# A four-layer graph attention kernel: other all-node row blocks in layer 2, and the start of layer 3 tied behind layer 2's last row

## The chip, the cores and the metric

The kernel runs on one core of one Trainium2 chip. The metric is device time in microseconds (us) of one execution. Five engines work side by side, each in the order of its own instruction queue: PE (TensorE, matrix products), ACT (ScalarE, exponentials and copies), DVE (VectorE, elementwise work), POOL (GpSimd, which here issues gathers) and SP (SyncE, which issues plain DMAs). An instruction whose input is not there yet holds up everything behind it on the same engine.

## The reference

There are 4096 nodes with 256 features, an adjacency matrix with a density of about 1/256 plus the diagonal, and four graph attention layers. Each has a residual and a layer norm:

```
x = layernorm(x + layer_n(x, adj))          # n = 0, 1, 2, 3
layers 0, 1:  4 heads of 64;  layer 2: 2 heads of 128 (with biases)
   h = x W^T;  e[i,j] = leaky_relu(s1[i] + s2[j]) where adj[i,j], else excluded
   out[i] = softmax_j(e[i,:]) @ h
layer 3:  one score; softmax of e and softmax of -e (negated), both @ x,
   concatenated, @ fc_W, then elu
```

## The kernel before, in words

**Rows and tiles.** A tile of nodes is 128 rows, so there are NT = 32 row tiles, called row 0 to row 31 here. For each layer, a *projection* (class `Projection`, L526) turns a finished row into what the next layer needs of it: a value row for each node (`vals`) and its score terms (`edge`), both stored to DRAM. Its steps are a transpose on PE (`transpose`, L535), a copy of it on ACT (`copy`, xT, L543), the product on PE (L552), the scaling on ACT and DVE (`row`, L563, stored at L580), a transpose of the score terms (`edge`, L582) and their store (L588).

**Sparse rows.** Most row tiles are done sparsely (class `RowTile`). During layer 0 the kernel works out, for every row tile, a list of the neighbours that it has (`lists`), at most 13 x 128 of them, with packed masks (`maskC`). In every layer, a row tile then gathers 13 x 128 value rows with 13 indirect DMAs on POOL (L636), and its own 128 rows with a plain DMA on SP (L633). These 14 positions form two *halves* of seven (`half`, L640). Masked attention weights are made on ACT and DVE for each, and PE multiplies them with the gathered values (L711 in layers 0 and 1, L714 in layers 2 and 3). The lists are ordered so that the first six gathers touch only nodes of rows 0 to 16 (`MIX` = 17, `FRONT` = 6). The first half of a row tile of layer n+1 thus needs only the projections of rows 0 to 16; its second half needs those of all 32 rows. Gathered data goes to slots of two pools, `g0` (16 slots) and `g1` (14 slots). In layer 3 a position takes a whole slot, and in the other layers two positions share one. First halves use `g0`, and second halves `g1` (`place`, L609).

**All-node rows.** Some blocks of four row tiles are not done sparsely but against all 32 node tiles (`whole_rows`, L908). `WHOLE` (L98) gives the number of such blocks in each layer: three in layer 2 (rows 20 to 31) and one in layer 3 (rows 28 to 31). They are always the last blocks. One *unit* is the work of one block with one node tile: an exponential on ACT and a mask on DVE for 128 x 512 weights, and the matmuls (L953). Layer 2 has 96 units of two heads, layer 3 has 64 units of one sign each. Units need no gathers, only value rows and a mask read in order, so they are spread between the sparse halves. `whole` (L769) issues units in proportion to the half-steps done so far. The full masks of these blocks are saved in DRAM (`maskW`) by one store of 2.16 MB for each block (L392), while layer 0 runs.

**The order of the work.** The program is written out once in Python. The order in which it issues is the order of each engine's queue, except where the tile framework's scheduler moves instructions by their priority; `issue_after` makes it place instructions after a named one. In layers 2 and 3 a half-step (`half_with_whole`, L825) does the transpose of at most one finished row, a half of the current sparse tile, the rest of that projection, and its share of units. Finished rows wait in `ready`, in the order in which `norm` (L975) finishes them. `GROUPS` (L76) says how many consecutive rows share one layer-norm chain.

**The border of two layers.** `close` (L863) ends a layer. It projects those rows below 17 that are still in `ready`, asks for the gathers of the next layer's first tile, finishes the layer's last row, issues the first half of the next layer's tile 0, projects the remaining rows, and then handles the loads of tiles 1, 2 and 3 and the first half of tile 1. The next layer's first gather on POOL waits for the value stores of rows 0 to 16 and for free slots; the first gather of a second half waits for the stores of all rows.

**Banks.** PSUM is split into `ptwo` (two pairs), used for the sparse accumulators and for the projections of layers 1 and 3, and `pfour`/`pthree`, turns over the other banks, used for the units' accumulators and for the projections of layer 2.

Of the kernel before, what the change touches and what calls it, by code (L numbers as in the profile page):

```python
# [45 lines left out]
ALU = mybir.AluOpType  # L46
# [4 lines left out]
P = 128  # L51
N = 4096
F = 256
NT = N // P
KT = F // P
BT = 4
W = BT * P
NB = NT // BT
# [14 lines left out]
CAP = NG * P  # L73
HALF = NP // 2

GROUPS = (((24, 4),), ((28, 2),), ((16, 2), (20, 1), (31, 2)), ((28, 1), (31, 4)))  # L76
LEAD = 10
MIX = 17
FRONT = 6
# [15 lines left out]

WHOLE = (0, 0, 3, 1)  # L98

LEAST = 2.0611536224385579e-09  # L100

# [76 lines left out]
class Turns:  # L178


    def __init__(self, pools):
        self.pools = list(pools)
# [6 lines left out]
class Program:  # L189
# [98 lines left out]
    def lists(self, ctx):  # L288
# [75 lines left out]
        class Block:  # L364
# [23 lines left out]

            def places(self):
                blk = self.blk  # L390
                if blk >= NB - max(WHOLE):
                    nc.sync.dma_start(out=shared["maskW"][blk], in_=self.mk)  # L392
                hit = wk.tile([P, BT, NT], BF16, name="hit")
                nc.vector.tensor_scalar(hit, self.red, 0.0, None, op0=ALU.is_gt)
                flat = hit.rearrange("p t j -> p (t j)")
                nc.vector.memset(flat[:, blk * BT:blk * BT + (BT - 1) * (NT + 1) + 1:NT + 1], 0.0)
                pt = prog.bank(prog.pthree)
                nc.tensor.matmul(pt[:, :P], flat, ones, start=True, stop=True)
                totals = wk.tile([P, P], BF16, name="totals")
                nc.scalar.copy(totals, pt[:, :P])  # L400
                pq = prog.bank(prog.pthree)
                nc.tensor.matmul(pq[:, :P], tri, flat, start=True, stop=False, skip_group_check=True)
                nc.tensor.matmul(pq[:, :P], totals, bt.rearrange("p t j -> p (t j)"), start=False, stop=False,
                                 skip_group_check=True)
                nc.tensor.matmul(pq[:, P:P + BT], totals, tot, start=False, stop=True, skip_group_check=True)
                ms = slice(blk * BT, (blk + 1) * BT)
                self.place = wk.tile([P, BT, NT], F32, name="place")
                here = self.place
                nc.vector.tensor_tensor(here, pq[:, :P].rearrange("p (t j) -> p t j", t=BT), lo[:, ms, :],
                                        op=ALU.subtract)  # L410
                nc.vector.tensor_tensor(here, here, hit, op=ALU.mult)
                nc.vector.tensor_copy(total[:, ms], pq[:, P:P + BT])

                for col in (wid[:, ms, :], None):
                    off = wk.tile([P, BT, NT], F32, name="off")
                    if col is None:
                        nc.vector.tensor_scalar(off, here, 0.0, None, op0=ALU.is_lt)
                    else:
                        nc.vector.tensor_tensor(off, here, col, op=ALU.is_gt)
                    nc.vector.tensor_tensor(bad, bad, off, op=ALU.max)  # L420
# [105 lines left out]
class Projection:  # L526
# [54 lines left out]

    def edge(self):  # L582
        self.pe = self.prog.bank(self.banks[2])
        self.nc.tensor.transpose(self.pe[:TERMS[self.n], :P], self.terms[:, 0, :], self.shared["ident"])

    def store(self):
        n, nc, T = self.n, self.nc, TERMS[self.n]
# [12 lines left out]
class RowTile:  # L600

    def __init__(self, layer, m):
        self.layer, self.m = layer, m
        self.slots = {}
        self.accs = None

    def place(self, pos):  # L609


        L, n = self.layer, self.layer.n
        per = 1 if n == 3 else 2
        s = pos // per
        if s not in self.slots:
            pool = L.prog.g1 if n > 0 and s * per >= HALF else L.prog.g0
            self.slots[s] = pool.tile([P, 2 * ROW[0]], F32, name="G")
        c = (pos % per) * ROW[n]
        return self.slots[s][:, c:c + ROW[n]]
# [20 lines left out]
    def half(self, half):  # L640
# [1 line left out]
        prog, sh, S = L.prog, L.shared, self.S  # L642
        H, Wd, V, T, A = HEADS[n], WIDTH[n], VALS[n], TERMS[n], LOGS[n]
        if self.accs is None:
            pool = prog.ptwo[1 if n == 3 and self.m % 2 else 0]
            self.accs = [prog.bank(pool) for _ in range(2 if n == 3 else 1)]
        accs = self.accs
        G = [self.place(half * HALF + k) for k in range(HALF)]
# [88 lines left out]
class Layer:  # L737
# [2 lines left out]

    def __init__(self, prog, n):
        self.prog, self.n, self.nc, self.shared = prog, n, prog.nc, prog.shared
        self.count = NT - WHOLE[n] * BT
        self.tiles = {}
        self.loaded = set()
        self.units = self.whole_rows()
        self.total = WHOLE[n] * NT * (1 if n < 3 else 2)
        self.used = 0
        self.nxt = self.middle = self.stored = self.between = None
        self.group = []  # L750
        self.ready = []
        self.step = 0
        self.last = ()


    def tile(self, m):
        if m not in self.tiles:
            self.tiles[m] = RowTile(self, m)
        return self.tiles[m]

    def load(self, m, half):
# [4 lines left out]
    def set_banks(self):  # L766
        self.prog.banks = self.prog.ptwo[1] if self.n in (0, 2) else self.prog.pthree

    def whole(self, step):  # L769

        while self.between is None and self.used < self.total \
                and self.used < self.total * (step + 1) / (2 * self.count - 6):
            next(self.units)
            self.used += 1
        if self.used == self.total:
            next(self.units, None)

# [15 lines left out]
    def half_alone(self, m, part):  # L793


        self.step = 2 * m + part
        proj, middle = None, self.middle
        second = m > NT - (LEAD if self.n == 0 else 6) and len(self.ready) > 1
        if self.ready and self.ready[0][0] < self.step and (part == 0 or second):
            self.set_banks()  # L800
            if part == 1 and self.n == 0:
                self.prog.banks = self.prog.pthree
            proj = Projection(self.prog, self.n + 1, self.nxt, *self.ready.pop(0)[1:])
            proj.transpose()
        if part == 1 or self.tile(m).accs is None:
            self.tile(m).half(part)
        if self.stored is not None:
            self.stored.store()
        if proj is not None:
            proj.copy()  # L810
        if part == 0 and m >= 1:
            self.tile(m - 1).copy()
        if proj is not None:
            proj.multiply()
        if part == 0 and m >= 1:
            self.tile(m - 1).back()
        if middle is not None:
            middle.row()
        if part == 1 and m >= 1:
            self.tile(m - 1).finish()  # L820
        if middle is not None:
            middle.edge()
        self.stored, self.middle = middle, proj

    def half_with_whole(self, m, part):  # L825

        proj = None
        self.step = 2 * m + part
        if self.ready and self.ready[0][0] < self.step:
            _, y, row = self.ready.pop(0)  # L830
            self.set_banks()
            proj = Projection(self.prog, self.n + 1, self.nxt, y, row)
            proj.transpose()
        with ExitStack() as order:
            for ins in self.last:
                order.enter_context(self.prog.tc.issue_after(ins))
# [3 lines left out]
        if self.between is not None:  # L840

            self.last = self.between()
            self.between = None
        if self.stored is not None:
            self.stored.store()
            self.stored = None
        if proj is not None:
            proj.copy()
            proj.multiply()
        if part == (0 if self.n == 3 else 1) and m >= 1:  # L850
            self.tile(m - 1).finish()
        self.whole(2 * m + part)
        if proj is not None:
            proj.row()
            proj.edge()
            self.stored = proj

    def steps(self):
        for m in range(self.count):
            for part in range(2):  # L860
                self.part(m, part)

    def close(self, following):  # L863

        last = self.count - 1
        self.step += 2
        if self.stored is not None:
            self.stored.store()
        if self.middle is not None:
            self.middle.row()  # L870
            self.middle.edge()
# [3 lines left out]
            self.set_banks()  # L875
            Projection(self.prog, self.n + 1, self.nxt, *entry[1:]).all()
        if following is not None:
            following.load(0, 0)
        if WHOLE[self.n]:
            for _ in self.units:  # L880
                pass
            self.tile(last).finish()
            if following is not None:
                following.tile(0).half(0)
        else:
            self.set_banks()
            first = Projection(self.prog, self.n + 1, self.nxt, *self.ready.pop(0)[1:])
# [7 lines left out]
            self.tile(last).finish()  # L895
            first.edge()
            first.store()
        for _, y, m in self.ready:
            self.set_banks()
            Projection(self.prog, self.n + 1, self.nxt, y, m).all()  # L900
        if following is not None:
            for m in (1, 2):
                following.load(m, 0)
# [4 lines left out]
    def whole_rows(self):  # L908
        n, nc, prog, sh = self.n, self.nc, self.prog, self.shared
        H, Wd, T = HEADS[n], WIDTH[n], TERMS[n]  # L910
        groups = [range(H)] if n < 3 else [(0,), (1,)]
        for blk in range(NB - WHOLE[n], NB):
            tiles = range(blk * BT, (blk + 1) * BT)
            S = prog.bk.tile([P, T, BT, P], F32, name="Sw")
            for it, m in enumerate(tiles):
# [59 lines left out]
    def norm(self, y, m):  # L975
# [24 lines left out]
            nc.vector.tensor_scalar(u, u, -0.5, 1.5, op0=ALU.mult, op1=ALU.add)  # L1000
            nc.vector.tensor_tensor(r, r, u, op=ALU.mult)
        for i, (y, m) in enumerate(self.group):
            nc.vector.tensor_scalar(y, y, mv[:, i, 0:1], r[:, i:i + 1], op0=ALU.subtract, op1=ALU.mult)
            dst = self.prog.out if self.n == 3 else self.shared["x"][self.n + 1]
            nc.sync.dma_start(out=dst[m * P:(m + 1) * P, :], in_=y)
            if self.n < 3:
# [498 lines left out]
```

## Time and profile before

| what | value |
|---|---|
| median of 3 runs | 2269.56 us (2267.93 to 2270.27) |
| the profiled execution's own time | 2264.38 us |
| its span in the profile | 2262.6 us |
| mean granted TensorE clock | 0.963 |
| PE busy | 2017.9 us (89%) |
| DVE busy | 1786.5 us (79%) |
| ACT busy | 1733.8 us (77%) |
| POOL busy | 1501.8 us (66%), of it 1488.8 in 1456 gathers |
| DMA moved | 493.01 MB, 218 GB/s on average |

The span is that of one execution, from its first instruction to its last, and all times inside the profile count from its start. "Busy" is the sum of instruction times on one engine. Projection and lists of layer 0 fill the first part. The last gathers of layer 2 are issued at 1681.56 us, the first of layer 3 at 1739.22 us. In the view of waits, a line reads: engine, tile and line that waited, what released it, total us, how often, and the longest.

### The profile page before, as it was taken

What the parts mean: (1) busy time and instruction counts of PE and PEld (TensorE: products, weight loads), DVE (VectorE), ACT (ScalarE), POOL (GpSimd) and SP (SyncE); (2) the same over time, 40 slices, a digit from 0 to 9 for tenths busy, and PEclk for the clock granted to TensorE, in tenths of its full rate; (3) what the DMA queues carried; (4) which work ended last, traced back from release to release, by engine and by line L of the source; (5) the groups of instructions that cost most, each with busy time, mean ns of one, the idle gap of its engine ahead of it and who ended that gap; (6) DMA issues with size and microseconds to landing.
All of it is one profiled execution on the core that took longest, in us unless ns stands there. A gap on an engine that the chain in (4) does not pass through costs nothing.

```text
span 2262.6 us, 49121 instructions
## 1 busy us (share of the span) xinstructions
PE 2017.9 (89%) x15689; PEld 1834.8 (81%) x15689; DVE 1786.5 (79%) x5061; ACT 1733.8 (77%) x4977; POOL 1501.8 (66%) x1596
## 2 busy tenths in 40 slices
PE   4878888989999969998898898999998899999996
PEld 2658777878999859988888898989996688778885
DVE  2988899999999859988888886886975455575566
ACT  4778988988789849978888877987873666686664
POOL 2117556656777777777777777777751677777773
PEclk7999999999999979999999999999999999999998
DMA  8889778776466665665656656777764788888884
GB/s 281 260 262 330 243 221 297 246 240 226 143 172 190 180 192 173 182 180 166 180 168 170 179 169 184 215 221 228 219 200 147 244 262 281 267 269 272 268 248 139
DMA packets 250321, 493.01 MB, mean 218 GB/s; under 512 B 44385, under 2 KB 156610, under 8 KB 249666
## 3 DMA queue, kind: packets, MB, share of 16 engines
q0 software_dynamic: 81536, 245.30, 37.3%
q1 hardware_dynamic: 168514, 244.46, 33.6%
q8 instruction: 126, 2.06, 0.4%
q14 instruction: 145, 1.19, 0.2%
HBM read 437.05 MB, written 52.54 MB: 216 GB/s over the span
## 4 chain that ended last, share of the span: by engine, by line
PE 48%; DVE 18%; DMA 15%; ACT 8%; issue 7%; POOL 3%; SPq 1%; DVEq 0%; ACTq 0%; POOLq 0%
PE bank L714 15%; PE bank L711 15%; DMA G<-vals,idx 8%; PE bank L953 8%; DVE w L670 6%; PE bank L552 4%; PE bank L441 4%; ACT w L699 3%; POOL G L636 3%; DMA raw<-in_adjB_dram 3%; DVE w L691 2%; DVE oh L435 2%; DMA G<-vals 2%; ACT pw L942 1%; ACT mk L380 1%
## 5 line engine op out<-in xcount | busy, mean ns | idle before, releaser
L636 POOL DMA_INDIRECT G<-vals,idx x1456 | 1488.8, 1023 | 722.6 <-issue 236.1
L699 ACT ACTIVATE w<-S,G 128x128 f32<-128x128 f32 x3248 | 1001.8, 390 | 144.9 <-DMA G<-vals,idx 105.5
L711 PE MATMUL bank<-w,G 128*65 128x128 f32 x7168 | 838.9, 277 | 61.1 <-DVE w L670 60.9
L711 PEld LDWEIGHTS bank<-w,G 128*65 128x65 f32 x7168 | 799.7, 140 | 71.0 <-DVE w L670 69.9
L670 DVE SCALAR_TENSOR_TENSOR w<-w,bank 128x1792 f32<-128x1792 f32 x256 | 514.4, 2012 | 15.0 <-ACT w L699 12.6
L714 PE MATMUL bank<-G,w 128*128 128x257 f32 (+1 forms) x2688 | 495.4, 342 | 30.4 <-DVE w L679 14.2
L714 PEld LDWEIGHTS bank<-G,w 128*128 128x128 f32 x2688 | 435.4, 194 | 80.9 <-DVE w L679 16.9
L953 PE MATMUL bank<-vw,pw 128*128 128x129 f32 (+1 forms) x2048 | 299.3, 302 | 5.3 <-ACT zw L1017 2.7
L953 PEld LDWEIGHTS bank<-vw,pw 128*128 128x128 f32 x2048 | 275.0, 192 | 21.9 <-ACT zw L1017 3.1
L677 ACT ACTIVATE w<-S,G 128x128 f32<-128x128 f32 x392 | 138.1, 393 | 138.3 <-DMA G<-vals 74.3
L435 DVE TENSOR_SCALAR oh<-iota,place 128x256 bf16<-128x256 f16 (+2 forms) x992 | 222.5, 300 | 10.1 <-PE bank L441 9.9
L691 DVE TENSOR_TENSOR w<-S,G 128x256 f32<-128x256 f32 x384 | 151.6, 416 | 70.5 <-DMA G<-vals,idx 67.4
L441 PE MATMUL bank<-mk,oh 128*128 128x132 fp8e4 x2336 | 189.9, 225 | 15.9 <-ACT cm L448 7.8
L552 PE MATMUL bank<-wext,xT 128*128 128x268 f32 (+3 forms) x640 | 180.6, 415 | 21.5 <-ACT xT L543 18.7
L441 PEld LDWEIGHTS <-oh 128*128 128x128 bf16 x2336 | 145.5, 98 | 52.0 <-DVE oh L435 15.6
L380 ACT ACTIVATE mk<-raw 128x1024 uint8<-128x1024 int32 x128 | 130.5, 1051 | 30.3 <-DMA raw<-in_adjB_dram 28.5
L552 PEld LDWEIGHTS bank<-wext,xT 128*128 128x128 f32 x640 | 118.5, 202 | 42.7 <-ACT xT L543 22.8
L943 DVE SCALAR_TENSOR_TENSOR pw<-pw,mw 128x512 f32<-128x512 f32 x192 | 127.4, 689 | 15.2 <-ACT pw L942 14.3
L942 ACT ACTIVATE pw<-Sw,d 128x512 f32<-128x512 f32 x192 | 133.1, 710 | 7.5 <-DMA Sw<-edge 5.3
L950 DVE TENSOR_TENSOR pw<-pw,mw 128x512 f32<-128x512 f32 x64 | 43.9, 689 | 112.4 <-ACT pw L949 57.9
L701 DVE SCALAR_TENSOR_TENSOR w<-w,mk 128x896 f32<-128x896 f32 x80 | 86.7, 1087 | 48.8 <-ACT w L699 48.6
L448 ACT ACTIVATE cm<-bank 128x396 uint8<-128x396 f32 (+1 forms) x160 | 68.8, 452 | 45.7 <-PE bank L441 44.4
(130 smaller groups left out, 1534.5 us busy)
## 6 DMA issues: line engine op xcount, KB each, us to landing
raw<-in_adjB_dram SPq DMA_DIRECT2D x128, 512.0 KB
mk<-maskC SPq DMA_DIRECT2D x112, 231.0 KB
G<-vals,idx POOLq DMA_INDIRECT x1456
S<-edge SPq DMA_DIRECT2D x64, 256.0 KB
vw<-vals SPq DMA_DIRECT2D x96, 129.0 KB
xp<-y SPq DMA_DIRECT2D x96, 128.0 KB
y<-xp SPq DMA_DIRECT2D x96, 128.0 KB
mw<-maskW SPq DMA_DIRECT2D x20, 528.0 KB
```

The costliest lines, as they stand in the source:

```text
L380: nc.scalar.activation(mk[:, q:q + 2, :, :P], src, AF.Copy, scale=EDGE)
L435: nc.vector.tensor_scalar(oh[:, :n * P], iota[:, :n * P], self.place[:, it, j:j + 1], None, op0=ALU.is_equal)
L441: nc.tensor.matmul(accs[b][:, s * MC:(s + 1) * MC], oh[:, (k - a) * P:(k - a + 1) * P], mk[:, j, it, :].bitcast(FP8), start=touches[b][0] ...
L552: nc.tensor.matmul(pp[:, :c1 - c0], self.xT[:, k, :], wext[:, k, c0:c1], start=(k == 0), stop=(k == KT - 1 and brow is None))
L636: nc.gpsimd.indirect_dma_start(out=self.place(pos), out_offset=None, in_=sh["v"][n][:NODES[t], :], in_offset=bass.IndirectOffsetOnAxis(ap= ...
L670: nc.vector.scalar_tensor_tensor(pair, pair, LEAST, mh2, op0=ALU.max, op1=ALU.mult)
L691: nc.vector.tensor_tensor(w[h][:, k:k + 2, :], S[:, h:h + 1, :].to_broadcast([P, 2, P]), dd[:, :, V + T + h:V + T + h + 1].to_broadcast([P ...
L699: nc.scalar.activation(w[h][:, k, :], S[:, h, :], AF.Exp, bias=d(k, h))
L711: nc.tensor.matmul(accs[0][:Wd, h * P:(h + 1) * P], v, w[h][:, k, :], **how)
L714: nc.tensor.matmul(a, w[h][:, k, :], v, **how)
L942: nc.scalar.activation(p, S[:, h], AF.Exp, bias=d)
L953: nc.tensor.matmul(accs[it][:, c:c + Wd], p[:, it, :], v[:, c:c + Wd], start=(j == 0 and h == heads[0]), stop=(j == NT - 1), skip_group_ch ...
```

## The change

`WHOLE` becomes a list of blocks for each layer. Layer 2's all-node blocks are 3, 7 and 6 in this order (rows 12 to 15, 28 to 31, 24 to 27) in place of 5, 6 and 7; its sparse rows are now 0 to 11 and 16 to 23. `GROUPS` follows that order, and `maskW` is saved for blocks 3, 6 and 7. Layer 3's all-node block stays block 7. In `half_with_whole`, rows below 17 are projected before others, and once the layer's units are used up two rows may be projected in one half-step, in its last three tiles. In layer 3, slots now alternate between the two pools by tile, with the second and third pairs arranged so that four first halves can be loaded at once. `close` loads four first halves of layer 3, projects what is ready, issues five of layer 3's units ahead of the last row's finish, and ties tile 0's first half and five more units behind the last row's scaled result and its projection's last transpose. The other 54 units of layer 3 are spread as before.

```diff
-GROUPS = (((24, 4),), ((28, 2),), ((16, 2), (20, 1), (31, 2)), ((28, 1), (31, 4)))
+GROUPS = (((24, 4),), ((28, 2),), ((16, 2), (17, 1), (20, 2), (24, 1), (31, 2)), ((28, 1), (31, 4)))
-WHOLE = (0, 0, 3, 1)
+WHOLE = ((), (), (3, 7, 6), (7,))
+AHEAD = 10
+ORDER = tuple([m for m in range(NT) if m // BT not in w] for w in WHOLE)
...
-                if blk >= NB - max(WHOLE):
+                if any(blk in w for w in WHOLE):
                     nc.sync.dma_start(out=shared["maskW"][blk], in_=self.mk)
...
     def place(self, pos):
...
-            pool = L.prog.g1 if n > 0 and s * per >= HALF else L.prog.g0
+            if n == 3:
+                other = self.step % 2 == 0 if self.step > 3 else self.step > 1 and s < HALF
+            else:
+                other = n > 0 and s * per >= HALF
+            pool = L.prog.g1 if other else L.prog.g0
...
     def whole(self, step):
         while self.between is None and self.used < self.total \
-                and self.used < self.total * (step + 1) / (2 * self.count - 6):
-            next(self.units)
-            self.used += 1
+                and self.used < self.ahead + (self.total - self.ahead) * (step + 1) / (2 * self.count - 6):
+            self.unit()
...
     def half_with_whole(self, m, part):
-        proj = None
+        projs = []
         self.step = 2 * m + part
-        if self.ready and self.ready[0][0] < self.step:
-            _, y, row = self.ready.pop(0)
-            self.set_banks()
-            proj = Projection(self.prog, self.n + 1, self.nxt, y, row)
-            proj.transpose()
+        able = sorted((e for e in self.ready if e[0] < self.step), key=lambda e: e[2] >= MIX)
+        self.set_banks()
+        over = self.used == self.total and m > self.count - 4
+        for entry, banks in zip(able, (self.prog.banks, self.prog.pthree)[:1 + over]):
+            self.ready.remove(entry)
+            projs.append(Projection(self.prog, self.n + 1, self.nxt, *entry[1:], banks=(banks,) * 3))
+            projs[-1].transpose()
...
     def close(self, following):
...
         if following is not None:
-            following.load(0, 0)
+            for m in range(4 if following.n == 3 else 1):
+                following.load(m, 0)
         if WHOLE[self.n]:
             for _ in self.units:
                 pass
+            if following is None:
+                self.tile(last).finish()
+                return
+            following.ahead = AHEAD
+            self.project_ready()
+            for _ in range(AHEAD // 2):
+                following.unit()
             self.tile(last).finish()
-            if following is not None:
+            scaled = self.scaled
+            proj = self.project_ready()
+            with ExitStack() as order:
+                for ins in (scaled, proj.last):
+                    order.enter_context(self.prog.tc.issue_after(ins.ins))
                 following.tile(0).half(0)
+                for _ in range(AHEAD - AHEAD // 2):
+                    following.unit()
...
-        for blk in range(NB - WHOLE[n], NB):
+        for blk in WHOLE[n]:
```

`project_ready` projects all rows in `ready` one after the other and gives back the last projection; its `last` is the transpose of the score terms in `edge`, and `self.scaled` is the last instruction of `norm` that scales a row.

## The prediction

> **What bounds the kernel now.** I read the page first, then the windows around the border between layers 2 and 3, where the diff acts, then the chain of waits there, then POOL's timeline. The page's busy totals and two rows of its slices:
>
> ```profile
> PE 2017.9 (89%) x15689; PEld 1834.8 (81%) x15689; DVE 1786.5 (79%) x5061; ACT 1733.8 (77%) x4977; POOL 1501.8 (66%) x1596
> ...
> PE   4878888989999969998898898999998899999996
> ...
> POOL 2117556656777777777777777777751677777773
> ```
>
> No engine is full over the whole span; the slices tell more. PE is near full from the middle on, but POOL, which does little but issue gathers, falls to 5 and 1 in slices 30 and 31 (56.6 us each, 1640 to 1753), the end of layer 2. The windows there (columns: length, busy and count of PE, PEld, DVE, ACT, POOL, granted clock, DMA share, GB/s):
>
> ```profile
> 1700.00:1720.00 20.00, 20.00 (x155) 19.01 (x154) 19.93 (x114) 7.20 (x25) 0.00 (x0) 1.00 0.34 102
> 1720.00:1740.00 20.00, 16.56 (x91) 12.98 (x90) 10.05 (x50) 3.55 (x12) 0.78 (x1) 0.92 0.36 110
> 1740.00:1760.00 20.00, 12.96 (x49) 9.62 (x50) 6.11 (x16) 11.40 (x29) 14.21 (x16) 0.82 0.82 268
> ...
> 1780.00:1800.00 20.00, 11.15 (x40) 8.73 (x39) 5.21 (x8) 11.94 (x26) 15.18 (x16) 0.83 0.78 243
> ...
> 2040.00:2200.00 160.00, 160.00 (x741) 140.24 (x740) 95.95 (x285) 104.03 (x220) 123.84 (x119) 1.00 0.85 265
> ```
>
> PE is full to 1720 and has holes to 1800; the DMA engines are a third used while POOL is still, four fifths once it gathers. Two waits of 1690 to 1830 and POOL's timeline:
>
> ```profile
> POOL G L636 <- DMA y<-xp: 56.7, 1, 56.7
> ACT w L677 <- DMA G<-vals,idx: 27.9, 23, 6.0
> ```
>
> ```profile
> 1681.56 0.95 POOL L636 DMA_INDIRECT G<-vals,idx  x1 [0.30 <-issue]
> 1739.22 0.94 POOL L636 DMA_INDIRECT G<-vals,idx  x1 [56.72 <-DMA y<-xp]
> 1740.47 0.95 POOL L636 DMA_INDIRECT G<-vals,idx  x1 [0.30 <-issue]
> ```
>
> POOL stands 56.7 us. The releaser named, a load of y, was long done; what comes just before 1739.22 is the value store of node row 16, issued at 1735.38 (L580). Layer 3 has 28 sparse tiles of 13, 364 gathers, from 1739.22 to 2234.4: 1.36 us each, where 0.95 busy and 0.30 issue give 1.25. In 2040 to 2200 it is 160/119 = 1.345 with PE full too, so gathers and PE run in step and neither makes up a late start. After the last gather 28.2 us remain. Layer 3 ends a fixed stretch after its gathers get under way.
>
> PE's holes at the border, off its timeline: between 1728.14 and 1754.22, while projections run singly, 1.07, 0.52, 0.95, 0.52, 0.95, 0.52, 2.23, 2.97 and 0.41; then 0.89, 7.65 and 1.72 to 1800.52: 20.4 in all. The lower clock adds some 5.6: a projection's multiply (L552) took 3.46 and 3.81 us for 2.01, a half's matmuls (L714) 8.58 for 6.23.
>
> **What the Trainium skill says.** "TensorE: Matmul & The Clock Gate", What's actually happening: throttled is the default, and activity releases the clock. The trace agrees: 0.82 and 0.83 in the windows with holes, 1.00 in full ones. "Perfetto Trace Analysis", DMA Instruction — SWDGE (GPSIMD): a gather's profiled end is that of descriptor writing, not of the data. The trace agrees: bars of 0.95 us, landings 3.2 to 5.8 us after issue. "DMA: Bandwidth & Descriptors", Issuing engines are not separate DMA queues: SP's and POOL's transfers share 16 engines. That bears on the moved mask store below; the trace's share of 0.99 there fits.
>
> **The change part by part.** Sums are on the profiled execution, 2264.4 us (span 2262.6); the median of 2269.56 is 5.2 above it.
>
> *Early rows first.* A layer-3 tile's first six gathers touch node rows 0 to 16 only. Rows 12 to 15 now belong to layer 2's first unit block, and projections of rows under 17 go ahead of others, so row 16's store comes before the last sparse tiles instead of after them. 24 gathers (first halves of four tiles, two in each slot pool) now stand ahead of the first full-range one: 24 x 1.25 = 30 us into POOL's hole of 56.7. What hides them is that hole and the DMA share of 0.34; without it they'd cost what they cost now. They wait for slots that layer 2 frees tile by tile, the last three for its last half.
>
> *Two projections a step.* After the last layer-2 unit (1700.1) both orders have six sparse halves (3.13 us of PE each) and ten projections (2.07 each). Before, four lie between the halves, and the last half ends 28.0 us on. Now seven lie between: about 28.0 + 3 x 2.07 = 34.3, so 1734.3, or 1736.9 with a few short xT waits of 0.5 to 1 us. Then three projections (6.2) and five layer-3 units (1.735 each, 8.7), which fill the last row's finish (5.1 to 5.4 us on DVE, PE idle before). The last row's edge transpose, call it t, comes at about 1750 if nothing stalls.
>
> *What queues behind the tie.* ACT has tile 0's and 1's relus (L677), which wait for gathers as late as the 22nd and for own rows over SP, ahead of the last xT copies; DVE has a mask of tile 1 ahead of the last row's reciprocal and eight unit multiplies (0.69 each) ahead of its value product; PE has five units ahead of its transposes. Behind all three waits row 23's projection, its store and the 25th gather, the first that may touch any row. A relu waited up to 6.0 us here, and a copy held so left PE idle 2.97. Bounds 0 and 8.5 us (6.0 and a multiply or two queue): t is 1750 to 1758.5. I take 1757.5; a hold is likely.
>
> *From t on.* The store and issue took 3.8 us (1735.38 to 1739.22), so the 25th gather is at about t + 3.5, against 1775.99. Gathers 27 to 54 then wait for the halves of tiles 0 and 1 to free slots: half 6.1, five units 8.7, half 6.1 give t + 21; gathers of tile 1's second half to t + 27, landing 4 to 5, masks 2.3 and half 6 give about t + 40; seven more gathers at 1.25 put the 55th at t + 46 to 49, I take 46.4, against 1816.4. Gain: 1816.4 - 1750 - 46.4 = 20.0, or 11.5 with t = 1758.5, 12.5 with 1757.5. The 310 gathers left at 1.353 (460 us / 340 in 1776 to 2236) are 419, with the tail 28: t + 494. PE has 56 x 6.07 + 59 x 1.735 = 442 left after t, and with the 15 us tail ends by t + 457 plus its idle (32 of 493 us before): no later.
>
> *Steady layer 3.* Slots alternate by tile, not by half, with a look-ahead of two tiles as before. 54 units over 50 steps for 64: ten units, 17 us of PE, leave the stretch. If PE paces it, up to -5; if smaller units interrupt more, +3. I take 0.
>
> *The mask store* (L392, 2.16 MB) of block 5 at 372 us becomes one of block 3 at about 200:
>
> ```profile
> 200.00:220.00 20.00, 18.10 (x172) 17.04 (x170) 19.42 (x66) 15.76 (x43) 15.43 (x16) 0.91 0.99 326
> 220.00:240.00 20.00, 13.80 (x145) 13.36 (x143) 12.92 (x39) 16.24 (x41) 9.69 (x11) 0.83 0.99 353
> ```
>
> The engines are full there and DVE loses 7 us in the second window, waiting for raw loads and what follows. 2.16 MB at 340 GB/s is 6.4 us; queued ahead of a raw load on SP, it delays all of it or, hidden, none. At 372 DVE idled 2.7 us, regained. Net -2.7 to +6.4; I take +2.5.
>
> *Other order.* Unit weights of layer 2 now start from rows 12 to 15, so eight exponentials (0.71 on ACT) and multiplies (0.69 on DVE) move some tiles earlier at layer 1's end, where both engines have them to do anyway: 0, within 2 either way. The other norm groups have the same rows: 0.
>
> Sum: -12.5 + 2.5 + 0 = -10, so 2254.4 profiled and 2259.5 median.
>
> **Rivals.** *The hole closes wholly:* nothing holds t (1750), the mask store is hidden and the clock stays up: -20 to -25, about 2247. For it: DMA share 0.34 and PE full to 1720; against it: relus and copies in one queue.
>
> *The gain is eaten:* t near 1765, or t as taken and the mask store at its full price with 3 to 5 us lost in the paced halves: within 0.2% (4.5 us, about what this kernel's measurement can tell from no change), 2268. For it: the seven gathers of each half must land before its relus, twice in a row.
>
> *Slower:* the tie itself. If each of the three holds behind one another (own row over SP, 22nd gather, units' multiplies) costs the 8.1 us that DVE waited for ACT's pw here at the longest, t is 1750 + 24.3 = 1774. From t = 1770 the 55th gather is no earlier than before; 4 us beyond, with the store's 2.5, gives +6.5: 2276. For it: three engines wait in order; against it: 24 gathers need only 30 us of the hole.
>
> *It doesn't happen:* front gathers stay behind the last tile's slots, POOL's hole stays 50 us or more. Gathers 1 and 2 have free slots, so only partly; it ends as the second rival.
>
> **How the numbers follow.** My case 0.50 (-4.5 to -18), hole closed 0.20, eaten 0.14, slower 0.16. The range runs from just past the closed hole, 2244, into the slower case, 2273; my case alone is 2252 to 2265. Faster 0.70, same 0.14, slower 0.16.
>
> **What would show it.** Right: POOL busy over 10 us in the 20 us windows of 1700 to 1740; the 25th gather at 1753 to 1762; the 55th at 1796 to 1805; PE holes between 1728 and 1800 under 10 us; steady gathers still 1.35 apart; the last gather 28 us before the end. Wrong: ACT's relu waits ahead of an xT copy over 6 us; raw waits over 6 us longer at 200 to 240; or a stretch before 1680 that shifts by more than 4 us.

## The result

The changed kernel takes 2261.25 us (median of 7 runs, 2253.32 to 2264.68). The kernel before took 2267.40 us in the runs beside it (median of 7, 2263.02 to 2270.27). The ratio is 0.9973, with a 95% interval of 0.9959 to 0.9987: faster by 0.27%, or 6 us, where 10 were forecast. The two profiled executions differ by 3.1 us (spans of 2262.6 and 2259.5). Single executions of one kernel lie up to 9 us from their median here, so one pair of traces shows where time went, and the medians show how much.

The page of the changed kernel, with the rows that were shown of the kernel before:

```profile
PE 2020.2 (89%) x15689; PEld 1842.9 (82%) x15689; DVE 1786.0 (79%) x5061; ACT 1730.1 (77%) x4977; POOL 1493.1 (66%) x1596
...
POOL 2107656656667777777777777777773477777773
```

The work is the same, but POOL's hole has moved its weight: 7, 3 and 4 in slices 30 to 32 for 5, 1 and 6. The windows at the border, with the columns as in the prediction:

```profile
1700.00:1720.00 20.00, 18.05 (x129) 16.56 (x128) 19.55 (x98) 18.98 (x51) 6.78 (x8) 1.00 0.76 221
1720.00:1740.00 20.00, 15.39 (x96) 13.50 (x95) 11.03 (x56) 4.41 (x15) 5.62 (x6) 0.91 0.70 199
1740.00:1760.00 20.00, 17.19 (x87) 14.68 (x86) 12.88 (x39) 9.44 (x18) 1.93 (x3) 0.91 0.51 146
1780.00:1800.00 20.00, 19.66 (x91) 16.96 (x90) 9.99 (x13) 17.29 (x37) 13.52 (x13) 1.00 0.77 238
2040.00:2200.00 160.00, 149.59 (x675) 128.63 (x674) 93.43 (x284) 98.95 (x214) 124.04 (x119) 0.99 0.83 253
```

From 1740 on PE is fuller than before (17.19 for 12.96, 19.66 for 11.15). Between 1700 and 1740 it is emptier (33.4 us busy for 36.6), although it has more to do there. In 2040 to 2200 it is no longer full, yet the same 119 gathers are issued: 1.345 us each, as before. The waits of 1690 to 1830, and POOL's timeline around the first gather that may touch any row:

```profile
POOL G L645 <- PE bank L723: 30.4, 23, 9.6
ACT w L686 <- DMA G<-vals,idx: 30.0, 16, 6.6
...
POOL G L645 <- DMA vals<-row: 22.9, 1, 22.9
```

```profile
1743.91 0.95 POOL L645 DMA_INDIRECT G<-vals,idx  x1 [0.30 <-issue]
1767.78 0.94 POOL L645 DMA_INDIRECT G<-vals,idx  x1 [22.93 <-DMA vals<-row]
```

The single wait of 56.7 us has become some twenty for slots (released by matmuls of layer 2), and one of 22.9 us for the last row's value store. *Front gathers* are here the 24 of the first halves of tiles 0 to 3, which touch rows 0 to 16 only; a *full-range* gather may touch any row. All 24 front gathers are out at 1743.91; the 25th gather, the first full-range one, waits for the store alone.

In the kernel before, POOL's timeline has the first full-range gather in 21st place, with four front gathers behind it that are issued before the 25th:

```profile
1770.85 1.08 POOL L636 DMA_INDIRECT G<-vals,idx  x1 [4.24 <-issue]
1775.99 0.95 POOL L636 DMA_INDIRECT G<-vals,idx  x1 [0.30 <-issue]
```

No releaser is named, but POOL's queue stood there in a wait of 8.8 us that ended at 1770.14, 4.1 us after the last row's value store was issued. The last edge transposes of the two kernels, on PE, first before and then changed:

```profile
1765.83 0.27 PE L584 MATMUL bank<-ident,row 128*1 128x128 f32 x1
1764.09 0.27 PE L587 MATMUL bank<-ident,row 128*1 128x128 f32 x1 [0.95 <-DVE row L581]
```

The last row's projection itself thus came only 1.7 us earlier.

The gather stream allows a simple account, which I use for every run below. It counts layer 3's gathers 1 to 364 in the order of POOL's queue and calls the last gather of layer 2 gather 0. *Border* is the time from the start of gather 0 to the start of the 25th, *stream* from there to the start of the last gather, *tail* from there to the end of the span. All three come from POOL's timelines of single executions.

| kernel | border | stream | tail | sum |
|---|---|---|---|---|
| before | 94.4 | 457.5 | 29.2 | 581.0 |
| changed | 86.8 | 457.6 | 34.1 | 578.5 |

The border gave 7.6 us. The stream did not move at all: in both kernels POOL waits only 3.5 and 6.2 us in it beyond the 0.30 between two gathers, so the issue of gathers itself sets its length. The tail took 4.9 us back. Kernels with the same order of work differ by 2 to 3 us in their border (experiments 2 and 8), so these are sizes to within about that. The two sums differ by 2.5 us of the 3.1; the rest lies ahead of gather 0. The eight kernels of the first chips that have the changed order of layer 2 issue gather 0 at 1674.6 to 1682.6, on average 2.7 us before the 1681.56 of the one trace of the kernel before; whether a part of the gain in the medians lies there, no run separates.

### The profile page after: what moved, and what is told of

Its sections match the earlier page's. It is cut to its first block, busy times and chain, and to the rows that moved or that the text cites. A ratio compares the mean times of both kernels' runs of the same rounds, so it can differ in the third digit from the quotient of the medians.

```text
span 2259.5 us, 49108 instructions
## 1 busy us (share of the span) xinstructions
PE 2020.2 (89%) x15689; PEld 1842.9 (82%) x15689; DVE 1786.0 (79%) x5061; ACT 1730.1 (77%) x4977; POOL 1493.1 (66%) x1596
## 5 line engine op out<-in xcount | busy, mean ns | idle before, releaser
L686 ACT ACTIVATE w<-S,G 128x128 f32<-128x128 f32 x392 | 137.2, 391 | 148.6 <-DMA G<-vals 94.6
L688 DVE TENSOR_TENSOR w<-w,mk 128x896 f32<-128x896 f32 x56 | 61.0, 1090 | 96.3 <-ACT w L687 87.6
```

The lines of the kernel that those rows point to most:

```text
L686: nc.scalar.activation(w[0][:, k, :], S[:, 0, :], AF.Relu, bias=d(k, 0))
```

## The experiments

All kernels were timed beside the kernel before on the same chip, so two kernels are compared by their ratios to it. The first eight ran on chips where that took 2267.05 and 2267.08 us. The last four ran on one where it took 2768.77; they are told apart below. "No difference" means that the intervals, 2 to 5 us either way, overlap.

**1. Tile 1's relus behind the last projection.** ACT's timeline of the changed kernel shows what the last projections met (L686 are relus of layer 3, L573 the exponential of a projection's row, L546 a projection's copy):

```profile
1723.29 0.40 ACT L686 ACTIVATE w<-S,G 128x128 f32<-128x128 f32 x1 [4.28 <-DMA G<-vals,idx]
...
1734.16 0.40 ACT L686 ACTIVATE w<-S,G 128x128 f32<-128x128 f32 x1 [5.05 <-DMA G<-vals,idx]
1734.47 0.45 ACT L573 ACTIVATE row<-bank 128x2 f32<-128x2 f32 x2
```

A relu of tile 1 stands for 4.28 and again for 5.05 us until its gather has landed, and the rows of two projections go right after it, at 1734.47. The gather it waits for is itself late, since its slot comes free with layer 2's halves. The tie of the change holds tile 0's half on DVE and PE only: an instruction is placed behind a named one on that one's engine, and the two named are on DVE and PE. Tile 0's relus and their two followers indeed stand on ACT from 1710.58 on, ahead of all these projections. Tile 1 isn't tied at all. The edit, all else as changed:

```diff
-        nc.scalar.activation(vals[:, :, D:], sc[:, 2 * T:2 * T + H].rearrange("p (h o) -> p h o", o=1), AF.Exp)
+        self.exp = nc.scalar.activation(vals[:, :, D:], sc[:, 2 * T:2 * T + H].rearrange("p (h o) -> p h o", o=1), AF.Exp)
...
+        tied = ()
...
+                tied = (scaled, proj.last, proj.exp)
...
-            following.tile(1).half(0)
+            with ExitStack() as order:
+                for ins in tied:
+                    order.enter_context(self.prog.tc.issue_after(ins.ins))
+                following.tile(1).half(0)
```

> The changed kernel with layer 3's tile 1 tied behind the last row's projection on ACT, DVE and PE (nothing is left out). Theory (in-order holds): tile 1's relus, which wait for late gathers, stood in ACT's queue ahead of the last four projections and made layer 2's last halves and the last edge transpose some 10 to 14 us late (1764.1 instead of about 1750). Without them PE's holes of 3.5 and 2.8 us before 1750 go, the last edge transpose comes at 1752 to 1757, the first full-range gather at 1756 to 1761 instead of 1767.8, and the end is 5 to 10 us earlier than the changed kernel (some 2252 to 2256). Rival (gathers or the SP queue pace layer 3 whatever the border does): the border moves but the end stays within 2 us of the changed kernel. Second rival: the relus' 5 us of ACT work are then exposed after the last row, and the first gather gains under 4 us.

Measured: 2249.02 us, ratio 0.9922 (0.9905 to 0.9939), against the changed kernel's 0.9973. In its account the border is 79.6, the stream 456.7 and the tail 34.2. POOL's timeline:

```profile
1735.15 0.94 POOL L645 DMA_INDIRECT G<-vals,idx  x1 [0.30 <-issue]
1754.56 0.94 POOL L645 DMA_INDIRECT G<-vals,idx  x1 [18.47 <-DMA vals<-row]
```

Counted from gather 0 (1674.91 here, 1681.02 in the changed kernel), the last edge transpose comes at 76.1 us instead of 83.1, and the 25th gather moves by the same 7.1. The stream passes it on to the end in full. The holes of 3.48 and 2.81 us that PE had in the changed kernel before 1750 are gone too. So the hold is shown, and its price is 7 us of the border; the medians differ by some 12, of which the trace accounts for 7.9. Both rivals fall.

**2. Output stores behind the own-row loads.** The tail of the changed kernel, on PE, on SP and in ACT's waits of 2200 to 2220:

```profile
2216.82 26.77 PE L723 MATMUL bank<-G,w 128*128 128x257 f32 x112 [7.80 <-ACT z L1057]
```

```profile
2204.14 0.34 SPq L1045 DMA_DIRECT2D out_dram<-y  x1
2204.65 0.90 SPq L642 DMA_DIRECT2D G<-vals  x2
```

```profile
ACT w L686 <- DMA G<-vals: 8.6, 1, 8.6
```

The last four halves run in one piece, 7.80 us late. They wait for the accumulators' copy z on ACT, and ACT and DVE had stood on a relu that waited 8.6 us for its tile's own rows. That load is issued at 2204.65, right behind an output store (2204.14) that had waited for DVE. All through layer 3 ACT's relus wait longest for own rows. The edit keeps a store back and places it behind the next own-row load; no matmul and no gather changes place:

```diff
-                nc.sync.dma_start(out=self.place(pos), in_=sh["v"][n][m * P:(m + 1) * P, :])
+                L.own = nc.sync.dma_start(out=self.place(pos), in_=sh["v"][n][m * P:(m + 1) * P, :])
...
+            self.flush()
...
+    def flush(self):
+        if self.late:
+            with self.prog.tc.issue_after(self.own.ins):
+                for m, y in self.late:
+                    self.nc.sync.dma_start(out=self.prog.out[m * P:(m + 1) * P, :], in_=y)
+        self.late = []
...
-            nc.sync.dma_start(out=dst[m * P:(m + 1) * P, :], in_=y)
+            if self.n == 3 and self.late is not None:
+                self.late.append((m, y))
+            else:
+                nc.sync.dma_start(out=dst[m * P:(m + 1) * P, :], in_=y)
```

> The changed kernel with each layer-3 output store put behind the next own-row load on SP; no other queue moves (nothing is left out). Theory (own rows held on SP): in layer 3 an own-row load stands behind an output store that waits for DVE, ACT's relus wait for it (94.6 us between 1820 and 2235), and the last four halves start 8 us late. Without it these waits fall below 50 us, the 7.8 us hole of PE at 2209 to 2217 goes, the last gather to the end is about 28 us again instead of 33, and the whole is 4 to 8 us faster than the changed kernel. Rival (the own row is only the last named of several waits): the gathers pace the halves anyway, waits move to the gathers, and the time stays within 2 us.

Measured: 2254.56 us, ratio 0.9941 (0.9922 to 0.9959); the interval just touches the changed kernel's. The account: border 89.5, stream 457.6, tail 30.0. ACT's waits of 1820 to 2235, first of the changed kernel and then of this one:

```profile
ACT w L686 <- DMA G<-vals: 94.6, 17, 8.6
ACT w L686 <- DMA G<-vals,idx: 25.9, 32, 2.0
```

```profile
ACT w L686 <- DMA G<-vals,idx: 95.9, 102, 3.2
ACT w L686 <- DMA G<-vals: 23.0, 7, 5.7
```

The own-row waits fell to a quarter, and the waits for gathers rose by as much: 120.5 us in all before, 118.9 after. Inside the stream the rival is right: own rows were only the last named of two late inputs. In the tail the theory is right in size, 34.1 to 30.0, though PE still has a hole of 6.7 us there, where 7.80 was to go. The border's 89.5 for 86.8 is scatter: only SP's order differs. This profiled execution was itself the slowest but one of its kind (span 2258.4), so its sum shows 1.4 us where the medians show about 7.

**3. Both mends.** The two edits together.

> The changed kernel with both mends: tile 1 tied behind the last projection on all engines, and layer 3's stores put behind the next own-row load (nothing is left out). Theory: the two causes lie in different places (border, tail), so they add: ratio to the kernel before about 0.989 (0.986 to 0.992), some 2242 us. Rival (both only shift the same slack of the gather stream): no better than the first mend alone, 0.992.

Measured: 2246.68 us (2237.26 to 2247.56), ratio 0.9902 (0.988 to 0.9924): border 74.9, stream 458.5, tail 29.7. Both gains are there side by side, as the account says they must be when they lie before and behind a stream that doesn't move. This version beats both kernels, by 1% and 0.7%. That it beats the first mend alone is likely but not certain, since the intervals overlap.

**4. No units ahead.** `AHEAD = 0`: the border's ten units go back into layer 3's steps, though the scheduler still places four ahead of the last edge transpose (five in the changed kernel).

> The changed kernel with no layer-3 units at the border (all 64 spread over layer 3's steps as before; nothing is left out). Theory (ten units ahead are worth PE time in a stretch that PE paces): the first full-range gather comes 0 to 5 us earlier, since no units stand before the last transposes, but halves 20 to 40 of layer 3 fall back by up to 15 us against the changed kernel and its end is 3 to 8 us later. Rival (gathers pace layer 3): the end is within 2 us of the changed kernel, or up to 4 us earlier with the earlier gather.

Measured: 2258.17 us, ratio 0.9963 (0.9949 to 0.9976), no difference from the changed kernel. Border 86.4, stream 460.9, tail 31.7. The stream grew by 3.3, the tail shrank by 2.4. The rival holds: PE time in the middle of layer 3 shows no worth here.

**5. The old blocks.** `WHOLE = ((), (), (5, 6, 7), (7,))` with the old groups of layer 2.

> The changed kernel with layer 2's all-node blocks as before (rows 20 to 31; masks saved for blocks 5, 6, 7), all else as changed (nothing is left out). Theory: the gain needs rows 0 to 16 early; with row 16 the fourth last sparse tile its value store comes later, so fewer than 24 first-half gathers are issued before layer 2's last half; the mask store's delay of 2.9 us at 187 us goes, and the end is 2 to 6 us later than the changed kernel. Rival (early rows don't matter since the last row's store releases the full-range gathers in both): within 2 us of the changed kernel or, with the mask store gone, 2 us earlier.

Measured: 2259.28 us, ratio 0.9967 (0.9954 to 0.998), no difference. Border 84.0, stream 455.0, tail 31.7. POOL's timeline shows why:

```profile
1686.46 1.44 POOL L645 DMA_INDIRECT G<-vals,idx  x1 [0.30 <-issue]
1730.58 0.94 POOL L645 DMA_INDIRECT G<-vals,idx  x1 [42.68 <-DMA vals<-row]
```

The hole is back, 42.7 us of it, and yet the 24 front gathers are all out at 1760.4, ten before the 25th follows at 1770.5. They need to be out by then and no earlier; how full POOL's hole is ahead of that made no difference.

**6. One projection a step.** `over = False`.

> The changed kernel with at most one projection in a half-step to the end of layer 2 (nothing is left out). Theory (the gain comes from having fewer projections left, run singly, after layer 2's last half): three more projections follow the last half one by one, each with PE idle about 2 us, so the first full-range gather comes 4 to 8 us later than in the changed kernel and the end 3 to 7 us later, near the kernel before. Rival: with tile 1's relus holding ACT anyway, the second projection of a step was held too, and nothing changes (within 2 us).

Measured: 2255.45 us, ratio 0.9949 (0.9932 to 0.9966); border 88.6, stream 458.1, tail 32.9. It isn't slower, and may be faster. The theory that pairs of projections carry the gain falls.

**7. No tie.** The loop over `(scaled, proj.last)` runs over nothing.

> The changed kernel without the tie: layer 3's tile 0 first half and five units are placed by the scheduler alone (nothing is left out). Theory (the tie keeps 6.1 us of half and 8.7 us of units out of the way of the last row's projection): the last edge transpose comes up to 15 us later, the first full-range gather with it, and the end is 5 to 10 us later than the changed kernel. Rival (the work is only reordered, PE stays filled, and tile 0's slots come free earlier for gathers 27 to 33): within 2 us of the changed kernel.

Measured: 2253.70 us, ratio 0.994 (0.992 to 0.996); border 83.2, stream 456.0, tail 35.6. Tile 0's half now starts at 1754.84, ahead of the last edge transpose (1759.00), and the kernel isn't slower, perhaps 0.3% faster. The theory that the tie helps falls too.

**8. One load ahead.** `range(1)` in place of `range(4 if following.n == 3 else 1)`.

> The changed kernel with the first half of only tile 0 loaded at the border ahead of the last projections, as before the change (nothing is left out). Theory (24 gathers in POOL's hole are worth their time): fewer gathers stand ahead of the first full-range one, some of their 1.25 us each come back after the last row's store, and the end is 4 to 9 us later than the changed kernel. Rival (tile 1's gathers then come later but its relus hold the projections less or not at all): equal or up to 6 us earlier.

Measured: 2260.22 us, ratio 0.9972 (0.9962 to 0.9982); border 89.2, stream 458.6, tail 32.9. This edit tests nothing. The scheduler gave PE, ACT and POOL the very same order, and only a few waits on DVE and loads on SP differ. It serves as a repeat of the changed kernel: 0.9972 for 0.9973, and its border shows that 2 to 3 us in the account are scatter.

**9 to 12, on the other chip.** There the kernel before took 2768.77 us, so only comparisons inside this group hold. The page of one of them (the kernel before with the stores moved) shows the difference:

```profile
L711 PE MATMUL bank<-w,G 128*65 128x128 f32 x7168 | 951.1, 289 | 242.9 <-issue 217.7
L699 ACT ACTIVATE w<-S,G 128x128 f32<-128x128 f32 x3248 | 999.5, 389 | 252.6 <-PE bank L711 172.8
```

One ACT operation takes 389 ns, as on the first chips (390), but PE stood 217.7 us ahead of L711, the matmuls of layers 0 and 1, for nothing that the profile shows. Two more things set these four apart. The stream takes 502 to 506 us, and POOL waits 49 to 56 us in it beyond the 0.30, where that was 3 to 7 us in all ten kernels of the first chips; so here the issue of gathers alone doesn't pace layer 3. And single executions scatter widely ahead of the border: gather 0 stands at 2124.9 and at 2140.6 in two of these kernels whose layers 0 to 2 are the same.

*The old slot places* (`place` as before, all else as changed):

> The changed kernel with the slot places of before (first halves in one pool, second halves in the other; nothing is left out). Theory (the slot places carry the border's gain: they let all 24 first-half gathers go before the last store, so that the first full-range gather waits for the store and not for its turn): gathers 15 to 24 must again wait for the halves of tiles 0 and 1, the first full-range gather comes 6 to 15 us later than in the changed kernel counted from layer 2's last gather (94 us and more instead of 87), and the time is back at the kernel before or above it (ratio 0.999 to 1.004). Rival (projections in pairs, early rows and units ahead carry it together): within 2 us of the changed kernel.

Measured: ratio 0.9977 (0.9964 to 0.999). Only 14 front gathers stand ahead of the first full-range one, which starts 91.2 us after gather 0; the other ten follow behind, and the 25th is at 103.7, each 1.25 us after the last. Its border is 2.4 us longer than that of the kernel before with the stores moved (101.3), and still the kernel is faster than the one before there. Its trace doesn't put that gain at the border or behind it: from gather 0 to the end it takes 643.2 us, and the other three, all made from the kernel before, take 637.1 to 638.9.

*The new slot places alone*, in the kernel before:

> The kernel before with the new slot places of layer 3 alone (nothing is left out). Theory: the front gathers no longer stand behind tile 0's and 1's halves; the first full-range gather comes right after the last store, 5 to 8 us earlier (about 88 us after layer 2's last gather), and the ratio to the kernel before is 0.997 (0.995 to 0.998), all of the change's gain. Rival: the order of projections at the border is what counts, and the ratio is 1.000 within 0.001.

Measured: ratio 1.0034 (1.0016 to 1.0052), slower. POOL did what was expected until the last store:

```profile
2217.59 0.94 POOL L640 DMA_INDIRECT G<-vals,idx  x1 [0.30 <-issue]
2231.85 0.94 POOL L640 DMA_INDIRECT G<-vals,idx  x1 [13.32 <-issue]
```

```profile
SPq L976 <- remote: 13.1, 1, 13.1
```

The 24 front gathers ran without a gap. But the last projection stood 13 us: PE for a copy on ACT, ACT until 2222.06 and SP until 2222.09, both for something that the profile gives only as "remote". Waits of that kind stand in all four traces of this chip and in none of the ten of the first chips, so they belong to this chip rather than to the edit. And the profiled execution took 2765.58 us, 12 less than its kernel's median and less than the median of the kernel before, so it can't show why the kernel is slower. The run doesn't say what the slot places are worth alone.

*Three more mask stores* in the kernel before, where the change has its one:

```diff
+                if blk == 3:
+                    for q in range(3):
+                        nc.sync.dma_start(out=shared["maskW"][q], in_=self.mk)
```

> The kernel before with three more mask stores of 2.16 MB, those of block 3's mask to three unused places, where the changed kernel has its one (nothing is left out). Theory as predicted: one such store costs about 2.5 us in the full DMA stretch, three 7 to 8, so a ratio of 1.003; at the full price of 6.4 each it is 1.008. Rival (layer 0 isn't paced by DMA there, and the 2 to 4 us by which the changed kernel lay back in layer 0 is the scatter of single executions): under 2 us for the three.

Measured: ratio 1.0006 (0.9986 to 1.0025). Three stores cost 1.7 us by the middle of the interval and at most 7, so one at most 2.3; nothing is clear of zero. The chip's layer 0 is slower, and the DMA engines may have more room there: with the three stores their share is 0.69 between 200 and 400 us, against 0.80 for the kernel before on the first chips. The single traces of the first chips show no cost either: in the run with the old blocks, which has no store of block 3, gathers lie back by 2.9 us at 309 us, as in the changed kernel, and in the first mend's, which has it, by 0.6.

*Stores behind own rows*, in the kernel before:

> The kernel before with layer 3's output stores put behind the next own-row load on SP (nothing is left out). Theory (the tail's 5 us came with the changed kernel: its PE ran ahead of the gathers and met the own-row wait at the end): the kernel before has a tail of 29 us already, so it gains 0 to 3 us, a ratio of 0.999 to 1.000. Rival (the own-row loop slows every tile of layer 3 in both kernels): 5 to 8 us, 0.997.

Measured: ratio 1.0001 (0.9985 to 1.0016): nothing to gain, as the theory had it, on this chip. On the first chips the changed kernel and its variants with the stores in place have tails of 31.7 to 35.6 us, for 29.2 in the kernel before. So the tail's loss came with the changed kernel; that the stores would not have helped the kernel before on those chips isn't shown.

## Why the prediction was right

The direction, the place and the main mechanism were right: the end follows the start of the gather stream, and the stream starts earlier. The first mend shows that link by itself. The size was 6 us for 10, inside the range, and part of that is luck. The last edge transpose came at 1764.1, as in the rival "the gain is eaten" (t near 1765, 2268 us) and not at the 1757.5 of the prediction's own case; the pair of traces gives 3.1 us, which is what that rival allows. Of the six signs that were to show it right two came: the gathers still 1.345 apart and PE's holes under 10 us. POOL's share of 1700 to 1740, the 25th gather (1767.78 for 1753 to 1762), the 55th (1812.18 for 1796 to 1805) and the last one (34.1 us before the end for 28) missed. A sign of being wrong, a shift of over 4 us before 1680, came too in this one trace (4.4 us near 230), though not in that of the first mend, whose order is the same there. By the prediction's own steps:

- **"Layer 3 ends a fixed stretch after its gathers get under way."** The stream is the best confirmed step. It lies between 455.0 and 460.9 us in all ten kernels of the first chips, whatever was done to units, stores or projections. The tail is not fixed: 29.2 before, 34.1 after. This term of the sum was taken as 0 and measured +4.9. PE got ahead of the stream (the 34th of layer 3's 56 halves ended 15.7 us earlier than before, while the 25th and the last gather were 8 us ahead), and the end then hung on an own-row load behind an output store on SP. The second mend removes it.
- **"Early rows first."** The 24 gathers did go into the hole. That their 30 us are a gain was the wrong account. In the kernel before, 20 front gathers stood ahead of the first full-range one and four behind it, so at most 4 x 1.25 = 5 us were to be had, and with the old blocks there was no difference.
- **"Two projections a step"** and its 1734.3 to 1736.9 for the last half's end: it ended at 1742.8. Relus held the rows of the pairs on ACT; the step missed that the hold begins before the last half and not only behind the tie. With one projection a step the kernel wasn't slower, so the step isn't shown to be worth anything by itself.
- **"What queues behind the tie."** The mechanism was named, its size was not: bounds of 0 to 8.5 us, 7.5 taken, and the last edge transpose came at 1764.1 instead of 1750, 14 us. Of these, 7 go when tile 1's relus go behind; the other 7 weren't taken apart.
- **"From t on"**: the 25th gather came 3.7 us after the transpose (3.5 said), the 55th 48.1 after it (46.4 said).
- **The border's sum** was -12.5, reckoned to the 55th gather, and measured -4.2 there (1812.18 for 1816.41). To the 25th, counted from gather 0, it is -7.6: 5.1 for the four front gathers, 1.2 for the last edge transpose, and 1.3 for the time from there to the first full-range gather (3.7 us for 5.0). The 30 gathers between took 44.4 us for 40.4.
- **"Steady layer 3: 0."** From the 25th gather to the last it measured +0.1, but from the 55th, where the prediction starts it, -3.8. With the tail's +4.9 that gives the -3.1 of the two traces.
- **"The mask store, +2.5"**: not shown. A kernel without it lay back by as much in layer 0, and one with it by 0.6.
- The windows of 1700 to 1740 have 6.78 and 5.62 us of POOL, not over 10 each: slots came free with the halves, one tile at a time. The holes of PE between 1728 and 1766 are 0.70, 0.44, 2.81, 0.85 and 0.95, 5.8 us in all, under the 10 forecast.
- One reading was a little off: in the trace the gathers' landings came 3.2 to 6.3 us after issue, not 3.2 to 5.8. Nothing in the sum rests on it.

What stays open is which part of the change carries the gain. Old blocks, one projection a step, no tie and fewer units ahead were each tried with all else as changed, and none lost it. Without the new slot places there was a gain too, but on the other chip, where its trace doesn't show it at the border, and the slot places alone couldn't be judged there. Several parts seem to stand in for one another: each brings the front gathers out before the last store, or the last store forward. That is argued from the account, not shown.

## What to carry to other kernels

Where a stream of gathers paces a stage (here POOL waited only 3 to 7 us in some 457 beyond its 0.30 between two), ask for two things first: when its first unrestricted gather may start, and how many restricted ones are still in the queue by then. Filling the hole ahead of that made no difference here. When work of the next stage is loaded early, look at what it puts into the in-order queues of other engines: an early relu waiting for a late gather cost 7 us here, and a tie must name an instruction on every engine that it is to hold. A gain at one end of a stage can be taken back at the other by a queue that was just hidden, so look at the tail as well as at the edited place.

## What the runs showed of the hardware

The same program took 2267 us on some chips and 2769 on another. Two profiles of the kernel before are compared here; the one of the other chip has the stores moved, which changes nothing in its time. Single ACT and DVE operations take the same on both (389 and 390 ns for the relu-sized exponential, 2015 and 2012 for the largest mask). PE is busy 236 us longer (2254.2 for 2017.9): its matmuls in layers 0 and 1 take 289 ns for 277, and the granted clock of the execution was 0.887 for 0.963. The rest of the 515 us between the two spans is time in which PE stands; ahead of those matmuls alone it stands 217.7 us without a cause that the profile shows. Most of the difference lies in layers 0 to 2: the last gather of layer 2 is issued at 2141 us instead of 1682, while from there to the end it takes 637 us instead of 581. Most gathers cost POOL 0.94 to 0.95 us and 0.30 between two on both, yet layer 3's stream took 504 us for 457, for there POOL waited 54 us in it, and 3.5 on the first. What made that chip slower stays open.
